# Attention and quantized feed-forward on one core: Newton steps of a layer norm on GpSimd, splits spread over the steps, a pool moved by 128 bytes

## The chip, the cores and the metric

The kernel runs on one core of a Trainium2 chip. The metric is the device time of one execution in microseconds, and a kernel is given by the median of its runs. In the text PE is TensorE (PEld its weight load), DVE is VectorE, ACT is ScalarE, POOL is GpSimd, SP is SyncE, which only issues DMAs here. L150 means line 150 of the kernel before.

## The reference

One transformer block on x [8, 128, 512] in float32: cross attention to a context of the same shape, then a gated feed-forward of 1376 hidden columns whose three weights are quantized to NF4 (4 bits, blocks of 64, scaled by the largest magnitude) and turned back first.

```python
x = x + xattn(layernorm(x), ctx, ctx, mask, Wq, Wk, Wv, Wo)   # 32 query heads, 8 key heads, 128 each,
                                                              # rope, 30 * tanh(logits / 30), softmax
n = layernorm(x)                                              # (x - mean) / sqrt(var + 1e-5), over 512
dq1, dq2, dq3 = (nf4_quant_dequant(w) for w in (w1, w2, w3))
h = silu(n @ dq1.T) * (n @ dq2.T)
out = x + h @ dq3.T
```

## The kernel before

The order of the instructions is written out by hand: each engine carries out its own in the order of the program text, and waits at semaphores for the others.

Every large product takes its float32 operands as two parts, `hi` and `lo`. `split` (L133) makes them: ACT casts `hi`, and DVE or POOL subtracts for `lo`. `product` (L144) then issues three matmuls for each pair, at L148, L149 and L150: hi by lo, hi by hi, lo by hi. The first operand of each is the stationary one.

The program has four stages. First come the keys and values of the context. Then the attention runs in 64 steps `i`, each for one batch and half of a key head's group. Step `i` projects step i-3 (`po`, added by DVE into `acc[b]` at L654; the PSUM buffer `wo` of `po` exists once), transposes and splits the result of step i-2 (`aT`), multiplies weights and values of step i-1 (`pv`, then DVE's reciprocal and `ad` at L642 and L643), and makes the scores of step i (`pl`, tanh and exp on ACT, mask product on POOL at L633).

The second layer norm lies among the last steps. `sums` gives mean and variance of a batch, `finish` the reciprocal root for a pair of batches, `rows` the normalized rows, `turned` transposes them into `xT2`. In `rsqrt` a first guess comes from a shift and a subtraction of the bits, and three Newton steps of three operations each, all on DVE (L100 to L105), on tiles of 128x2. For batches 0 and 1 `finish` and `rows` come at the end of step 60, for 2 and 3 at the end of step 62; batches 4 to 7 follow after the loop.

The feed-forward takes 22 tiles of 24 matmuls (`gate_up`): gate `pg` and up `pu`, for the two halves of the batches and 11 blocks of hidden columns. The first two are issued among the last of the attention; the others are the 20 steps `n` of a loop. Evacuating one means `sg` on ACT (Silu, L700) and `hT` on DVE (L701), one step later. Its weights come by DMAs that POOL's queue issues (`load_w12`, L677) into six buffers with the tag `wq`. The down product `pd` follows: for each batch, `hT` is split by `split_h` into tiles `hs` (also in the six `wq` buffers), four blocks of hidden columns at a time, and multiplied with `w3t`. The 24 splits are in the list `to_split`: three after the last `gate_up`, then one ahead of each of the following entries of `down`.

Beside all this runs a stream of small steps that quantizes the three weights (`quantize`): a POOL normalization (L184), 15 bounds (ACT L174, DVE L180), a last product on DVE (L215 or L257) and the split of the outcome (`store`). `pump(n)` issues as much of it as `n` DVE operations. From step 60 of the attention to the second step of the feed-forward loop none is issued. The tiles of `w3` are the last of the stream; `w3t_0` to `w3t_7` lie in the pool `f1` with `hT` and the output tiles `o`; `w3t_8` and `w3t_9` lie in `nf`, `w3t_10` in `xp`. `f1` is the last pool, and lies where the attention's own pool was.

```python
        if n == last:
            for _ in range(3):
                split_h(*to_split.pop(0))
```

Of the kernel before, what the change touches and what calls it, by code (L numbers as in the profile page):

```python
# [45 lines left out]
def tables():  # L46
    e = np.arange(0, HD, 2, dtype=np.float32)
    inv = (np.float32(1.0) / np.float32(10000.0) ** (e / np.float32(HD))).astype(np.float32)
    phase = np.arange(T, dtype=np.float32)[:, None] * inv[None, :]
    phase = np.tile(phase, (1, 2)).T  # L50
    cos, sin = np.cos(phase).astype(np.float32), np.sin(phase).astype(np.float32)
    sgn = sin.copy()
    sgn[:HD // 2] *= -1
    # A value is above a bound when their difference is above 0, and at most a bound when it is below
    # the next float. The factor makes each such difference larger than any step of the code.
    bias = np.array([np.nextafter(BOUNDS[i], np.float32(np.inf)) if i in NEG else -BOUNDS[i]
                     for i in range(15)] + [0], dtype=np.float32) * np.float32(BIG)
    return (np.ascontiguousarray(np.stack([cos, sgn])),
            np.ascontiguousarray(np.broadcast_to(bias, (P, 16))))
# [3 lines left out]
def block_kernel(ctx: ExitStack, tc: tile.TileContext, x, ctxt, mask, wq, wk, wv, wo, w1, w2, w3, w12t, w3_t,  # L63
# [23 lines left out]
    make_identity(nc, ident)  # L87
    # These bring TensorE to its full clock before the first loads are in.
    warm = bank("pv", "warm")
# [5 lines left out]

# [1 line left out]
    def rsqrt(v, y, n, name):  # L97
        i = tp.tile([P, n], I32, tag="rs_i", name=f"i_{name}")
        t = tp.tile([P, n], F32, tag="rs_t", name=f"t_{name}")
        V.tensor_single_scalar(i, v.bitcast(I32), 1, op=ALU.logical_shift_right)  # L100
        V.tensor_scalar(y.bitcast(I32), i, -1.0, float(0x5F3759DF), ALU.mult, ALU.add)
        for _ in range(3):
            V.tensor_tensor(t, y, y, ALU.mult)
            V.scalar_tensor_tensor(t, t, -0.5, v, ALU.mult, ALU.mult)
            V.scalar_tensor_tensor(y, t, 1.5, y, ALU.add, ALU.mult)  # L105

    class LayerNorm:
        """Of acc[b] for each b of bs: the sums of every b, then finish, then rows of every b."""

# [8 lines left out]

        def finish(self):
            n = len(self.bs)  # L120
            self.y = tp.tile([P, n], F32, tag="ln_y", name=f"y_{self.name}")
            v = tp.tile([P, n], F32, tag="ln_v", name=f"v_{self.name}")
            V.tensor_single_scalar(v, self.mv[:, :, 1], EPS, op=ALU.add)
            rsqrt(v, self.y, n, self.name)

# [5 lines left out]

# [1 line left out]
    def split(hi, lo, src, engine):  # L133
# [3 lines left out]
    def transposed(hi, lo, src, name, tag):  # L137
        """hi + lo = src [T, KT * P] with the columns on the partitions, [P, KT, T]. The split is returned."""
        pt = bank(tag, f"pt_{name}")
        for k in range(KT):  # L140
            E.transpose(pt[:, k * P:(k + 1) * P], src[:, k * P:(k + 1) * P], ident)  # L141
        return lambda: split(hi, lo, pt.rearrange("p (k t) -> p k t", k=KT), V)

    def product(out, pairs, start=True, stop=True):  # L144
        """out = the sum of lhsT.T @ rhs over pairs of (hi, lo), or a part of it."""
        n = len(pairs)
        for i, ((ah, al), (bh, bl)) in enumerate(pairs):
            E.matmul(out, ah, bl, start=start and i == 0, stop=False)  # L148
            E.matmul(out, ah, bh, start=False, stop=False)  # L149
            E.matmul(out, al, bh, start=False, stop=stop and i == n - 1)  # L150

# [1 line left out]
    def scales(a, r, w):  # L153
        """The largest magnitude of each block, and the factor that takes it to 1."""
        V.tensor_reduce(a, blocks(w), AX.X, ALU.max, apply_absolute_value=True)
        V.tensor_single_scalar(r, a, 2.0 ** -126, op=ALU.max)
        V.reciprocal(r, r)
# [4 lines left out]
    class Unit:  # L162
        """Up to 1024 columns of weights, with input channels on the partitions."""
        p = P
# [4 lines left out]
        def bound(self, i):  # L169
            """One more step of the code, from 0 to below, then its sign turned, then from 0 up. The sum is kept  # L170
            in PSUM: an operation of DVE with one operand there leaves GpSimd its port."""
            m = self.tile("nf_m", f"nm_{i}", BF16, 3)
# [16 lines left out]
    class Down(Unit):  # L189
        """Columns h0 to h1 of w3, from its transpose; w3_t has the rows of w3 in the order of (e, p), for 4 * p + e."""  # L190

# [33 lines left out]
    class Up(Unit):  # L225
        """Rows of w1 or w2 or both, from their transposes."""

# [4 lines left out]
        def parts(self, t):  # L232
            """Those of w1 and w2 in t."""
            n = KT * self.r
            return [(j, t[:, i * n:(i + 1) * n].rearrange("p (k h) -> p k h", k=KT)) for i, j in enumerate(self.js)]
# [32 lines left out]
    class Scales:  # L268
        """Those of 128 rows of w1 and of w2, which go to the rows of scale_d."""

# [27 lines left out]
    class Scales3:  # L298
        """Those of w3, of which four rows lie in a partition, a part at a time; and each to the rows of scale3_d
        for its 32 columns: an odd row begins in the middle of a block."""  # L300
        nb = 4 * H // BLK
# [36 lines left out]
    both = [Scales(h) for h in range(NHT)]  # L338
    # What is found in the course of each unit, and when.
    found = {0: [(6, both[2]), (12, both[3])]}  # L340
# [29 lines left out]
    def pump(n):  # L370
        """As much of the stream as n operations of DVE on 1024 columns."""
        credit[0] += n
        while credit[0] > 0:
            credit[0] -= next(stream, n + credit[0])
# [17 lines left out]
    with ExitStack() as c1:  # L392
# [6 lines left out]

# [1 line left out]
        raw_pool = []  # L401
# [12 lines left out]
        def columns(w, h, name):  # L414
            """The columns of one head of w, [P, 2, KT, HD]."""
            raw = stage(w[h], [P, KT, HD], name)
            t = wp.tile([P, 2, KT, HD], F32R, tag="wq", name=name, bufs=6)
            return t, lambda: split(t[:, 0], t[:, 1], raw, V if name == "wk_0" else Q)

        def rope(dst, src, cos, sgn, name, engine=None):  # L420
            """dst = src, in PSUM, turned by its positions; [P, 4, T]. The last step is returned."""
            hd = HD // 2
# [23 lines left out]

# [1 line left out]
        with ExitStack() as c3:  # L448
# [57 lines left out]
            def masks():  # L506
                """1 where a query attends; a query that attends nowhere weighs all keys alike."""
                mf = tp.tile([P, P], F32, tag="xn", name="mf")
# [18 lines left out]

            # The tiles of products, and what else is done in the slot of each.
            tiles = [("k", 0, 0), ("k", 1, 0), ("k", 2, 0), ("k", 0, 1), ("k", 1, 1), ("k", 2, 1),
# [6 lines left out]

            # Weights and context in the order of their use, with the slot that splits them.
            def load_tab(*_):
# [11 lines left out]
            def advance(n):  # L550
                """The splits of slot n, and loads for the next ones as their places come free."""
                while True:
# [47 lines left out]

# [1 line left out]
        at = c1.enter_context(tc.tile_pool(name="at", bufs=2))  # L602
# [67 lines left out]

# [1 line left out]
        w12, hT, ups = {}, {}, []  # L672
# [38 lines left out]
        for i in range(N):  # L711
# [24 lines left out]
            if i == 2:  # L736
                turn(0)
            if 0 <= i - 1:
                values(i - 1)
# [6 lines left out]
            if i in (60, 62):  # L746
                ln.finish()
                xn.update({k: ln.rows(k, ("xn", "t2")[k // 2]) for k in (i - 60, i - 59)})
            for k in due.pop(i, ()):
                todo[k]()  # L750
            if i >= 61:
                load_w12(i - 61)

        project(N - 3)
        turned((2,), "s")
# [20 lines left out]

    f1 = ctx.enter_context(tc.tile_pool(name="f1", bufs=2))
    w3t, hs = {}, {}

# [11 lines left out]
    for n, (half, h) in enumerate(order):  # L791
# [4 lines left out]
        if n in w12_at:  # L796
            load_w12(w12_at[n])
        if n == last:
            for _ in range(3):
                split_h(*to_split.pop(0))  # L800
    evac()
# [61 lines left out]
```

## Time and profile before

| | |
|---|---|
| runs | 811.72, 814.76 and 813.67 us; median 813.67 us |
| profiled execution, span | 813.2 us |
| profiled execution, own time | not listed apart from the span |
| granted TensorE clock, mean | 0.990 |
| busy, PE / DVE / ACT / POOL | 788.0 / 645.0 / 581.1 / 461.7 us |
| attention steps 60 to 63 | about 586 to 610 us |
| last `gate_up` matmul, first `pd` matmul | 740.54 and 743.41 us |

Times in the profile are microseconds from the span's start. A line of the timeline gives start, duration, engine, line, operation, output and inputs, and in brackets the idle time before it with what ended that. Durations of matmuls overlap, so the interval from start to start is the better measure of their pace. In a group's line, after the number of instructions, stand the busy time in all, the mean duration of one in ns, and the idle time before them with its releasers.

### The profile page before, as it was taken

How to read it: one execution, taken by the hardware profiler on the slowest of the kernel's cores; microseconds unless marked ns; L12 is line 12 of the kernel's file. 1: busy time of each engine (PE TensorE's matmuls, PEld its weight loads, DVE VectorE, ACT ScalarE, POOL GpSimd, SP SyncE). 2: the span in 40 equal slices, each digit the busy share in tenths (PEclk: the TensorE clock that was granted, in tenths of full speed). 3: DMA queues.
4: the chain of work that ended last, by engine and by line, in shares of the span. 5: the costliest groups of instructions: out<-in, count | busy, mean ns of one | idle time of the engine just before them, and what ended most of it. 6: DMA issues, size and time to landing. Idle time of an engine off the chain costs nothing.

```text
span 813.2 us, 11144 instructions
## 1 busy us (share of the span) xinstructions
PE 788.0 (97%) x3737; PEld 632.0 (78%) x3737; DVE 645.0 (79%) x876; ACT 581.1 (71%) x820; POOL 461.7 (57%) x370
## 2 busy tenths in 40 slices
PE   8997999999999999999999999999989999998998
PEld 6786877778777787787787887877768888886877
DVE  6748859988888888897888888879877788779941
ACT  6346758779787878888796978898732678669720
POOL 3466636577877777687787787887640223222100
PEclk9998999999999999999999999999999999999999
DMA  6966534736136444616326415331231344341011
GB/s 223 289 170 181 165 95 157 207 106 189 46 110 190 125 135 131 168 54 203 110 99 193 141 39 164 114 111 56 100 108 53 86 147 129 130 160 51 1 65 40
DMA packets 72167, 102.44 MB, mean 126 GB/s; under 512 B 6542, under 2 KB 41678, under 8 KB 72110
## 3 DMA queue, kind: packets, MB, share of 16 engines
q1 hardware_dynamic: 68942, 90.19, 36.3%
q0 software_dynamic: 3168, 11.54, 4.5%
q8 instruction: 30, 0.49, 0.3%
q14 instruction: 27, 0.22, 0.1%
HBM read 79.32 MB, written 22.38 MB: 125 GB/s over the span
## 4 chain that ended last, share of the span: by engine, by line
PE 74%; DVE 7%; DMA 6%; ACT 5%; issue 5%; POOL 2%; SPq 1%; DVEq 0%; POOLq 0%; ACTq 0%
PE po L150 7%; PE po L148 7%; PE po L149 7%; PE pq L148 7%; PE pq L150 7%; PE pq L149 7%; PE pv L640 6%; PE pl L627 6%; DMA s_w<-scale_d 4%; PE pt_a L141 3%; PE pd L150 3%; PE pd L148 3%; PE pd L149 3%; ACT nm_w L174 2%; PE pk L148 1%
## 5 line engine op out<-in xcount | busy, mean ns | idle before, releaser
L180 DVE SCALAR_TENSOR_TENSOR nc_w<-nm_w,nc_w 128x1024 f32<-128x1024 bf16 (+1 forms) x238 | 284.2, 1194 | 65.1 <-ACT nm_w L174 53.8
L174 ACT ACTIVATE nm_w<-w_w,bias 128x1024 bf16<-128x1024 f32 (+1 forms) x255 | 275.6, 1115 | 24.6 <-POOL w_w L184 20.1
L148 PE MATMUL po<-wo,aT 128*128 128x512 f32 x256 | 124.4, 486 | 3.2 <-DVE acc L654 2.4
L430 POOL TENSOR_TENSOR rs_q<-rs_q,sgnq 128x512 f32<-128x512 f32 x64 | 84.0, 1313 | 72.6 <-ACT rs_q L428 71.1
L633 POOL TENSOR_TENSOR th<-th,mt 128x512 f32<-128x512 f32 x64 | 83.7, 1307 | 41.4 <-ACT th L631 27.4
L148 PE MATMUL pq<-xT,wq 128*128 128x512 f32 x256 | 106.0, 414 | 0.3 <-DVE rc_q L429 0.3
L150 PE MATMUL po<-wo,aT 128*128 128x512 f32 x256 | 101.0, 395 | 2.5 <-DVE aT L135 2.5
L150 PE MATMUL pq<-xT,wq 128*128 128x512 f32 x256 | 100.2, 391 | 0.0
L149 PE MATMUL po<-wo,aT 128*128 128x512 f32 x256 | 99.9, 390 | 0.0
L149 PE MATMUL pq<-xT,wq 128*128 128x512 f32 x256 | 99.8, 390 | 0.0
L431 POOL TENSOR_TENSOR qr<-rc_q,rs_q 128x512 f32<-128x512 f32 x56 | 72.6, 1296 | 0.4 <-DVE rs L642 0.4
L640 PEld LDWEIGHTS pv<-vt,th 128*128 128x128 f32 x512 | 66.4, 191 | 4.9 <-POOL th L633 0.6
L148 PEld LDWEIGHTS po<-wo,aT 128*128 128x128 f32 x256 | 48.2, 188 | 27.3 <-issue 12.7
L640 PE MATMUL pv<-vt,th 128*128 128x129 f32 x512 | 67.6, 275 | 0.2 <-POOL th L633 0.2
L627 PE MATMUL pl<-qr,krt 128*128 128x512 f32 x128 | 65.6, 594 | 0.0
L149 PEld LDWEIGHTS po<-wo,aT 128*128 128x128 f32 x256 | 48.2, 188 | 22.0 <-issue 13.8
L427 ACT COPY rs_q<-pq 64x512 f32<-64x512 f32 x64 | 37.3, 582 | 39.2 <-PE pq L150 34.2
L184 POOL TENSOR_TENSOR w_w<-w_w,s_w 128x1024 f32<-128x1024 f32 (+1 forms) x17 | 39.8, 2343 | 44.7 <-DMA s_w<-scale_d 42.9
L630 ACT ACTIVATE th<-pl 128x512 f32<-128x512 f32 x64 | 38.4, 600 | 33.7 <-PE pl L627 33.3
L150 PEld LDWEIGHTS po<-wo,aT 128*128 128x128 f32 x256 | 48.0, 188 | 14.9 <-DVE aT L135 3.8
L150 PEld LDWEIGHTS pq<-xT,wq 128*128 128x128 f32 x256 | 48.0, 188 | 10.8
L148 PEld LDWEIGHTS pq<-xT,wq 128*128 128x128 f32 x256 | 48.2, 188 | 9.8 <-DVE rc_q L429 1.4
(140 smaller groups left out, 1723.6 us busy)
## 6 DMA issues: line engine op xcount, KB each, us to landing
s_w<-scale_d SPq DMA_DIRECT2D x60, 256.0 KB
w12t_d<-dqt SPq DMA_DIRECT2D x22, 512.0 KB
w<-w12t_d POOLq DMA_DIRECT2D x22, 512.0 KB, 4.6
raw_wq<-in_L_xattn_Wq SPq DMA_DIRECT2D x32, 256.0 KB
raw_wo<-in_L_xattn_Wo SPq DMA_DIRECT2D x32, 256.0 KB
ws<-in_L_ffn_w SPq DMA_DIRECT2D x20, 256.0 KB
w_w<-in_w12t SPq DMA_DIRECT2D x10, 512.0 KB
kr_d<-kr SPq DMA_DIRECT2D x16, 256.0 KB
```

The source lines that it names most:

```text
L148: E.matmul(out, ah, bl, start=start and i == 0, stop=False)
L149: E.matmul(out, ah, bh, start=False, stop=False)
L150: E.matmul(out, al, bh, start=False, stop=stop and i == n - 1)
L174: S.activation(m, self.w, AF.Relu, bias=bias[:self.p, i:i + 1], scale=BIG if up else -BIG)
L180: V.scalar_tensor_tensor(self.c, m, step, self.c, ALU.min, ALU.subtract if i == POS[0] else ALU.add)
L184: Q.tensor_tensor(self.w, self.w, self.s, ALU.mult)
L430: Q.tensor_tensor(s, s, every(sgn), ALU.mult)
L431: return lambda: (engine or Q).tensor_tensor(dst, c, s, ALU.add)
L627: E.matmul(pl, krt[kv, u % 2][:, bb * T:(bb + 1) * T], qr[u][:, bb].rearrange("p g t -> p (g t)"), start=True, stop=True)
L630: S.activation(th, pl, AF.Tanh, scale=ATTN_MULT / CAP)
L633: Q.tensor_tensor(em[i], em[i], mt.unsqueeze(1).to_broadcast([P, G, T]), ALU.mult)
L640: E.matmul(pv[:, g, :HD + 1], em[i][:, g], vt[kv][:, b], start=True, stop=True)
```

## The change

- `rsqrt` takes an engine. The shift and the subtraction stay on DVE; where the engine is POOL, each Newton step is four operations (square, times v, times -0.5 plus 1.5, times y), as against three on DVE.
- `finish` of batches 0 and 1 (step 60) and of 2 and 3 (step 62) runs its Newton steps on POOL. The rows of 0 and 1 move from the end of step 60 to step 61, ahead of `values(60)`; those of 2 and 3 from the end of step 62 to the place behind the loop, ahead of `project(61)`. Batches 4 to 7 stay as they were.
- In the feed-forward loop one `split_h` is issued at the end of each of the last four steps, in place of three at the end of the last.
- A tile of 128 bytes a partition, which nothing uses, is taken first from `f1`, so what else lies there moves by 128 bytes.
- Comments are left out.

```diff
-    def rsqrt(v, y, n, name):
+    def rsqrt(v, y, n, name, E=V):
...
         for _ in range(3):
-            V.tensor_tensor(t, y, y, ALU.mult)
-            V.scalar_tensor_tensor(t, t, -0.5, v, ALU.mult, ALU.mult)
-            V.scalar_tensor_tensor(y, t, 1.5, y, ALU.add, ALU.mult)
+            E.tensor_tensor(t, y, y, ALU.mult)
+            if E is V:
+                E.scalar_tensor_tensor(t, t, -0.5, v, ALU.mult, ALU.mult)
+                E.scalar_tensor_tensor(y, t, 1.5, y, ALU.add, ALU.mult)
+            else:
+                E.tensor_tensor(t, t, v, ALU.mult)
+                E.tensor_scalar(t, t, -0.5, 1.5, ALU.mult, ALU.add)
+                E.tensor_tensor(y, y, t, ALU.mult)
...
-        def finish(self):
+        def finish(self, engine=V):
...
-            rsqrt(v, self.y, n, self.name)
+            rsqrt(v, self.y, n, self.name, engine)
...
+            if i == 61:
+                xn.update({k: pair.rows(k, "xn") for k in (0, 1)})
             if 0 <= i - 1:
                 values(i - 1)
...
             if i in (60, 62):
-                ln.finish()
-                xn.update({k: ln.rows(k, ("xn", "t2")[k // 2]) for k in (i - 60, i - 59)})
+                ln.finish(Q)
+                pair = ln
...
+        xn.update({k: pair.rows(k, "t2") for k in (2, 3)})
         project(N - 3)
         turned((2,), "s")
...
     f1 = ctx.enter_context(tc.tile_pool(name="f1", bufs=2))
+
+    f1.tile([P, 32], F32, name="apart_2", bufs=1)
...
-        if n == last:
-            for _ in range(3):
-                split_h(*to_split.pop(0))
+        if n >= last - 3:
+            split_h(*to_split.pop(0))
```

## The prediction

> **What bounds the kernel now.** I read the page's busy shares first, then the stretches of ten microseconds, then each engine in order of time around both places that the change touches.
>
> ```profile
> PE 788.0 (97%) x3737; PEld 632.0 (78%) x3737; DVE 645.0 (79%) x876; ACT 581.1 (71%) x820; POOL 461.7 (57%) x370
> ```
>
> TensorE sets the time; only its idle places and its matmul interval can give time back. Its largest idle place among the stretches:
>
> ```profile
> 740.00:750.00 10.00, 6.33 (x20) 4.44 (x19) 9.69 (x12) 10.00 (x14) 2.20 (x2) 0.83 0.14 44
> ```
>
> Columns: length, then busy time and instructions of PE, PEld, DVE, ACT and POOL, the granted clock, DMA. PE is 3.7 us idle at clock 0.83 while ACT is full; from 720 to 730 ACT was busy for 2.04 us only. PE there, in order of time:
>
> ```profile
> 740.54 0.39 PE L150 MATMUL pu<-xT,w 128*128 128x512 f32 x1
> 743.41 0.47 PE L148 MATMUL pd<-w3t,hs 128*128 128x512 f32 x1 [2.48 <-issue]
> ...
> 745.31 0.76 PE L150 MATMUL pd<-w3t,hs 128*128 128x512 f32 x1 [1.20 <-DVE hs L135]
> ...
> 748.84 0.40 PE L149 MATMUL pd<-w3t,hs 128*128 128x512 f32 x1
> ```
>
> The down product (pd) starts late because the first `hs` casts come at the end of ACT's queue (742.70, below), and its third matmul waits for DVE's half. After that pause the matmuls from 745.87 to 748.43 start 0.43 us apart, at half the granted clock, where 0.23 is usual. The second idle place is the layer norm:
>
> ```profile
> 592.31 1.02 PE L627 MATMUL pl<-qr,krt 128*128 128x512 f32 x2
> 594.22 0.47 PE L148 MATMUL po<-wo,aT 128*128 128x512 f32 x1 [0.89 <-DVE acc L654]
> ...
> 595.65 0.50 PE L150 MATMUL po<-wo,aT 128*128 128x512 f32 x1 [0.73 <-DVE aT L135]
> ```
>
> ```profile
> 589.83 1.24 DVE L104 SCALAR_TENSOR_TENSOR t_y<-t_y,v_y 128x2 f32<-128x2 f32 x1
> ...
> 592.48 1.00 DVE L129 TENSOR_SCALAR xn_y<-acc,mv_y,y_y 128x512 f32<-128x512 f32 x2
> 593.40 0.68 DVE L654 TENSOR_TENSOR acc<-acc,po 128x512 f32<-128x512 f32 x1
> ```
>
> PE's projection waits for DVE's addition into `acc`, which stood behind the Newton steps (589.64 to 592.44) and two rows (1.0 us). The same comes again at 605.20 to 608.29.
>
> **Layer norm on GpSimd.** Off DVE go 9 instructions per finish at an interval of 0.195 us, one of which took 1.24 (it overlapped POOL's mask product, 589.77 to 591.06). The rows move behind the next step's `acc` addition and `aT` split. What is lost now: from pl to the third po takes 1.44 us in the undisturbed step 61 (587.26 to 588.70); here 3.34 (592.31 to 595.65) and 3.09 (605.20 to 608.29): 1.90 + 1.65 = 3.55 us.
>
> POOL gets 12 dependent operations of 128x2 per finish, which the trace lacks. Nearest rows:
>
> ```profile
> L633 POOL TENSOR_TENSOR th<-th,mt 128x512 f32<-128x512 f32 x64 | 83.7, 1307 | 41.4 <-ACT th L631 27.4 <-issue 12.7 <-DVE ad L643 1.0
> ...
> L184 POOL TENSOR_TENSOR w_w<-w_w,s_w 128x1024 f32<-128x1024 f32 x16 | 38.6, 2410 | 39.3 <-DMA s_w<-scale_d 37.5 <-DMA krt<-kr_d 1.8
> ...
> L618 POOL MEMSET vt<- 128x8 f32 x8 | 0.8, 114 | 8.3 <-PE pv L640 8.3
> ```
>
> A line through the first two leaves 0.20 us at no columns; one dependent pair at the start (memset to select, `ident`) shows 0.08 between. I take 0.26, so 3.1 us per finish. The ends are 0.11 (the memset: 1.4 us) and 1.24 (each blocked like that DVE operation: 14.9 us).
>
> First finish: POOL is free when mask product 60 ends, 591.06, and done at 594.2; by then DVE has done `acc` and `aT` and waits; rows 594.25 to 595.25, reciprocal and `ad` of step 60 (0.2 + 0.7) at 596.15. PE's next block, which ended at 598.06, ends at 596.04 without its stall and then wants that `ad`: 0.15 lost. Should POOL's next mask product (1.3 us) read first and block the rows, as a product blocked DVE at 589.83, about 1.1 us more is lost; I don't count it. Queued behind the rows on DVE are that `ad` and the next `acc`; behind the Newton steps on POOL the mask product of step 61, ready at 594.7 anyway, then the two w12 loads (1.25 us), needed only at 616. Second finish, in times 1.9 us earlier: DVE's three operations of it end at 602.3, POOL works to 605.4, the loads to 606.5, mask product 63 to 607.8; PE wants that at 607.7 (611.54 less 1.9 and 1.65, less the wait before it), so 0.2 lost with the wake-up. Gain 3.55 - 0.35 = 3.2 us; both finishes being last, it shrinks by 0.24 us for each 0.01 us more, to nothing at 0.26 + 3.2/24 = 0.39 us.
>
> GPSIMD Engine Reference, section "Engine selection", of the Trainium skill speaks against this: elementwise work with two inputs is about twice as slow there as on VectorE. An estimate by that page, twice DVE's 0.195, makes a finish 4.7 us and this part worth about 0.1 us, the total 3.1 us longer; no trace here shows these shapes on GpSimd.
>
> **One split per step.** ACT, in order of time:
>
> ```profile
> 734.53 0.63 ACT L700 ACTIVATE sg<-pg 128x512 f32<-128x512 f32 x1
> ...
> 742.70 1.65 ACT L134 CAST hs<-hT 128x512 fp32r<-128x512 f32 x3
> ```
>
> The loss now: without it the matmul at 748.84, eleventh of pd, would start at 740.54 + 0.23 + 10 x 0.232 = 743.09, so 5.75 us. Four splits (ACT 0.55 and DVE 0.6 each) go to steps 16 to 19; three stood after step 19. Neither they nor the rows issue a DMA. The first falls into ACT's 0.91 us gap before the sg at 721.81 and DVE's 4.67 us gap before 730.64, both of them waits of the NF4 stream and PE: nothing; without that gap it costs 0.55. The second lands before the sg at 734.53, which PE's last tile (first matmul 735.21) awaits: 0.55 lost. The third and fourth are needed 5.6 and 8.3 us after pd begins; DVE's queue, with one split ahead of each evacuation (735.78 + 0.6 + 0.6 + 3.8 + 0.6; then 0.6 + 3.8 + 0.6), ends them near 741.4 and 746.4. So pd starts at 741.3, with no clock loss: 5.75 - 0.55 = 5.2 us. Next late is `w3t_10`: its POOL half ends at 775.53, on a DVE queue whose work up to there is unchanged; pd needs it 150 matmuls in, at 776.2. Cover of 0.6 us, and it caps any faster pd.
>
> **The 128 bytes.** `apart_2` moves `w3t`, `hT`, `o`. In the program's placement `f1` begins at byte 155392 of a partition, the `wq` buffers with the stationary operand at 112768: 128 apart modulo 256, in pd as in the key product (`cT` also at 155392). The moving operand of gate and up (80000) is level with `wq` modulo 256. Intervals of starts in order of time: 0.232 in pd (749.08 to 764.88 holds 68), 0.231 in the key product, 0.227 in gate and up; `w3t_8` and `w3t_9`, in another pool (48512) and level, run at 0.227 within pd. That is a coincidence of four cases, no mechanism. After the move `w3t` is level too. Gain: 0.0055 x 150 = 0.8, capped at 0.65, and about 0.25 on the last two batches: 0.9 us. Its ends are 0 and 1.2; below zero only if level were worse, which gate and up exclude.
>
> SBUF — State Buffer, section "Who interferes with whom", of the Trainium skill says that PE never waits on anyone for SBUF. By that the move is worth 0 and the sum 0.9 us less.
>
> Comments removed: no instruction.
>
> **Sum.** 3.2 + 5.2 + 0.9 = 9.3. The profile gives no time of its own execution but the span, 813.2, which lies 0.5 under the median of the runs, 813.67 (811.72 to 814.76). Span 803.9; as a median 804.4.
>
> **Rivals.**
> - *GpSimd eats its gain* (0.39 us an operation or more, LN part near 0): 813.67 - 6.1 = 807.6. For it: unmeasured shape. Against: the 0.11 and 0.20 rows. 0.15.
> - *The NF4 stream does not come forward with PE.* The chain of waits runs in the feed-forward through scale DMAs (10.1 us), POOL's normalizing and ACT; if it kept its time, what the layer norm saves is lost at `w3t_10`: 807.6. Against: at 642.67 that chain stems from a PE matmul. 0.10.
> - *The splits do not come early*, as their `wq` buffers free late; with POOL at 0.39 us, no change: 812.7. Against: these held w12_8 and w12_9, last read at 718.9 and 729.8. 0.08.
> - *Slower:* DVE stands behind the rows for POOL and with it `ad`, `acc` and PE, twice. Each 0.1 us of operation above 0.39 costs 2.4 us, so it cancels the other 6.1 near 0.64 and is slower by 0.5% above 0.81; at 1.24 it loses 20 - 6 = 14 us: 828. For it: the 1.24 us collision. 0.05.
>
> **Numbers.** The forecast has 0.62. Half a percent, about what a measurement of this kernel tells from no change, is 4.1 us. Faster 0.62 + 0.15 + 0.10 = 0.87, same 0.08, slower 0.05. Range: best ends 3.55 + 5.75 + 1.2 = 10.5, so 803.2 less the runs' 1.2; up to the two 807.6 rivals plus 0.9: 802.0 to 808.5.
>
> **What would show it.** Right: POOL rows L103 and on at 128x2 near 0.2 us; no idle over 0.3 us before po after 592; pd's first matmul within 1 us of pu's last; clock 1.00 there; pd interval 0.227. Wrong: PE waiting for `ad` or `th` near 596 and 608 (GpSimd), for `w3t` before pd's 151st matmul (stream), or the time leaving faster than 809.6.

## The result, and the profile after

The changed kernel takes 805.01 us (median of 4 runs, 802.15 to 807.59) against 814.07 us (4 runs, 811.72 to 814.76) for the kernel before: ratio 0.9889, 95% interval 0.9868 to 0.9911, or 7.2 to 10.7 us. The four runs of the changed kernel lie in two pairs, 802.15 and 802.80 us and 807.22 and 807.59 us, and the slower pair has the lower granted clock (0.996 and 0.994 against 1.000 and 0.998). The profiled execution of the changed kernel took 807.22 us, with a span of 805.5 us. Its lines are numbered otherwise than those of the kernel before: `product` stands at L153 to L155, `split` at L139 and L140, the normalized rows at L134, the addition into `acc` at L659, `sg` at L705. The page gives the busy shares again:

```profile
PE 784.0 (97%) x3737; PEld 629.8 (78%) x3737; DVE 645.9 (80%) x858; ACT 580.7 (72%) x820; POOL 465.8 (58%) x394
```

The instruction counts are the change: 18 fewer on DVE, 24 more on POOL, none on PE. In the stretch that had held the largest idle place, PE is now full and its clock is whole (columns: length, then busy time and instructions of PE, PEld, DVE, ACT and POOL, clock, DMA):

```profile
730.00:740.00 10.00, 9.30 (x41) 7.39 (x40) 9.58 (x10) 10.00 (x13) 3.12 (x2) 1.00 0.11 42
740.00:750.00 10.00, 10.00 (x45) 8.27 (x45) 9.69 (x11) 9.31 (x13) 1.30 (x1) 1.00 0.17 55
```

PE in order of time, at the start of the down product, the changed kernel:

```profile
732.24 0.39 PE L155 MATMUL pu<-xT,w 128*128 128x512 f32 x1
733.32 0.50 PE L153 MATMUL pg<-xT,w 128*128 128x512 f32 x1 [0.70 <-ACT sg L705]
...
738.68 0.39 PE L155 MATMUL pu<-xT,w 128*128 128x512 f32 x1
738.91 0.39 PE L153 MATMUL pd<-w3t,hs 128*128 128x512 f32 x1
...
741.18 0.39 PE L154 MATMUL pd<-w3t,hs 128*128 128x512 f32 x1
...
772.68 0.39 PE L155 MATMUL pd<-w3t,hs 128*128 128x512 f32 x1
773.67 0.50 PE L153 MATMUL pd<-w3t,hs 96*128 96x512 f32 x1 [0.60 <-POOL w3t L140]
```

Between the last pu and the first pd there is no pause any more, and the eleventh pd (741.18) starts 2.50 us after the last pu, where it was 8.30 before. Two new waits stand in the same list: one for ACT's `sg` before the last gate-and-up tile (1.08 us from start to start where 0.23 is usual) and one for `w3t_10` (0.99). ACT in the same place shows why the first is there, a cast of `hs` between the last NF4 cast and `sg`:

```profile
731.27 1.09 ACT L139 CAST w3t<-w_w 128x512 fp32r<-128x512 f32 x1
732.17 0.62 ACT L139 CAST hs<-hT 128x512 fp32r<-128x512 f32 x1
732.69 0.58 ACT L705 ACTIVATE sg<-pg 128x512 f32<-128x512 f32 x1
```

In the layer norm the Newton steps are on POOL, 12 operations of 0.19 to 0.20 us, each starting 0.277 us after the one before. POOL in order of time, then DVE, then PE:

```profile
590.22 0.20 POOL L103 TENSOR_TENSOR t_y<-y_y 128x2 f32<-128x2 f32 x1
590.50 0.20 POOL L108 TENSOR_TENSOR t_y<-t_y,v_y 128x2 f32<-128x2 f32 x1
...
593.27 0.20 POOL L110 TENSOR_TENSOR y_y<-y_y,t_y 128x2 f32<-128x2 f32 x1
594.00 1.28 POOL L638 TENSOR_TENSOR th<-th,mt 128x512 f32<-128x512 f32 x1 [0.53 <-ACT th L636]
...
607.08 1.30 POOL L638 TENSOR_TENSOR th<-th,mt 128x512 f32<-128x512 f32 x1
```

```profile
590.40 0.69 DVE L659 TENSOR_TENSOR acc<-acc,po 128x512 f32<-128x512 f32 x1 [1.58 <-PE po L155]
...
593.51 2.06 DVE L134 TENSOR_SCALAR xn_y<-acc,mv_y,y_y 128x512 f32<-128x512 f32 x2 [0.89 <-POOL y_y L110]
595.49 0.17 DVE L647 RECIPROCAL rs<-pv 128x4 f32<-128x4 f32 x1
595.70 0.69 DVE L648 TENSOR_TENSOR ad<-pv,rs 128x512 f32<-128x512 f32 x1
...
605.86 2.81 DVE L134 TENSOR_SCALAR xn_y<-acc,mv_y,y_y 128x512 f32<-128x512 f32 x2 [0.77 <-POOL y_y L110]
```

```profile
591.53 1.02 PE L632 MATMUL pl<-qr,krt 128*128 128x512 f32 x2
591.99 0.80 PE L153 MATMUL po<-wo,aT 128*128 128x512 f32 x1
...
596.44 0.65 PE L146 MATMUL pt_a<-ident,ad 128*128 128x128 f32 x4 [1.11 <-DVE ad L648]
```

DVE's addition into `acc` no longer stands behind the Newton steps, and po runs on directly from pl: the old wait is gone. But the two rows take 2.06 us where they took 1.00. The second of them overlaps POOL's mask product (594.00 to 595.28), and PE waits 1.11 us for the `ad` behind them. The rows of batches 2 and 3 take even 2.81 us: the second of them overlaps the two w12 loads that POOL issues (605.76 to 607.06) and the mask product behind these (607.08 to 608.38).

**A ledger.** The time of TensorE's work is compared from the pl of step 60 on (it starts at 587.26 us before and 586.48 after): start of a matmul less the start of that pl, less the same in the profile of before. Earlier differences are left out because the granted clock drops to a half for stretches of 3.4 or 6.8 us near 8, 70 and 105 us, and how many there are differs between two executions of the same kernel: ahead of step 60 they sum to 13.7 us in the profile of before, and to 6.8 and 3.4 us in two profiles of the changed kernel. Whether the change has a part in that, no run shows. Minus is a gain, in us; "LN" is the first pt_y of batch 3 (612.67 us before), behind both finishes, "tile" the last pu matmul.

| kernel | LN | tile | 11th pd | 150th pd | 151st pd | end |
|---|---|---|---|---|---|---|
| changed | -1.96 | -1.07 | -6.87 | -7.67 | -6.91 | -6.93 |
| changed, a second profile | -1.97 | -1.65 | -7.45 | -8.25 | -8.12 | -8.01 |
| layer norm alone | -2.01 | -1.90 | -1.88 | -0.81 | -0.80 | -0.88 |
| splits alone | -0.01 | +0.69 | -5.05 | -4.93 | -4.71 | -4.70 |
| 128 bytes alone | 0.00 | +0.47 | +0.30 | -0.49 | -0.49 | -0.57 |
| changed, no bytes | -2.00 | -1.42 | -7.16 | -7.05 | -6.72 | -6.71 |
| 64 bytes | -1.98 | -1.59 | -7.33 | -7.20 | -7.20 | -7.43 |
| Newton on DVE | -1.78 | -1.03 | -6.83 | -7.62 | -6.81 | -6.75 |
| rows behind `ad` | -3.32 | -3.21 | -9.01 | -9.80 | -8.74 | -8.71 |
| rows behind `ad`, POOL halves | -3.33 | -2.89 | -8.69 | -9.49 | -9.49 | -9.59 |
| rows behind `ad`, splits ahead | -3.29 | -3.01 | -8.81 | -9.61 | -9.61 | -9.67 |
| all three | -3.30 | -2.65 | -8.45 | -9.25 | -9.25 | -9.31 |

Two profiles of one kernel agree to 0.01 us in the layer norm and differ by 0.6 us at the last tile and 1.1 us at the end. So the first column is good to hundredths, the last to about a microsecond. For the changed kernel it says 6.9 and 8.0 us; the medians say 9.1, with an interval that reaches down to 7.2.

### The profile page after: what moved, and what is told of

Its sections match the earlier page's. It is cut to its first block, busy times and chain, and to the rows that moved or that the text cites. A ratio compares the mean times of both kernels' runs of the same rounds, so it can differ in the third digit from the quotient of the medians.

```text
span 805.5 us, 11147 instructions
## 1 busy us (share of the span) xinstructions
PE 784.0 (97%) x3737; PEld 629.8 (78%) x3737; DVE 645.9 (80%) x858; ACT 580.7 (72%) x820; POOL 465.8 (58%) x394
## 4 chain that ended last, share of the span: by engine, by line
PE 70%; DVE 7%; issue 7%; DMA 6%; ACT 5%; POOL 3%; SPq 1%; POOLq 0%; DVEq 0%; ACTq 0%
PE po L155 7%; PE po L153 7%; PE po L154 7%; PE pq L153 7%; PE pq L155 7%; PE pq L154 7%; PE pv L645 7%; PE pl L632 6%; DMA s_w<-scale_d 4%; PE pt_a L146 3%; ACT nm_w L179 2%; POOL w3t L140 1%; DVE nc_w L185 1%; PE pd L153 1%; PE pk L153 1%
## 5 line engine op out<-in xcount | busy, mean ns | idle before, releaser
L153 PE MATMUL po<-wo,aT 128*128 128x512 f32 x256 | 125.1, 489 | 0.7 <-ACT th L635 0.7
L153 PE MATMUL pq<-xT,wq 128*128 128x512 f32 x256 | 106.0, 414 | 0.3 <-DVE rc_q L434 0.3
L155 PE MATMUL po<-wo,aT 128*128 128x512 f32 x256 | 100.8, 394 | 1.7 <-DVE aT L140 1.7
L155 PE MATMUL pq<-xT,wq 128*128 128x512 f32 x256 | 100.2, 391 | 0.0
L153 PEld LDWEIGHTS po<-wo,aT 128*128 128x128 f32 x256 | 48.2, 188 | 23.8 <-issue 12.9
L155 PEld LDWEIGHTS po<-wo,aT 128*128 128x128 f32 x256 | 48.0, 188 | 13.7 <-DVE aT L140 2.4
L155 PEld LDWEIGHTS pq<-xT,wq 128*128 128x128 f32 x256 | 48.1, 188 | 10.8
L153 PEld LDWEIGHTS pq<-xT,wq 128*128 128x128 f32 x256 | 48.2, 188 | 9.8 <-DVE rc_q L434 1.4
```

## The experiments

**The three parts, each alone.** The edit of each kernel is one part of the change put into the kernel before:

```
splits alone:      -        if n == last:              128 bytes alone:  +    f1.tile([P, 32], F32, name="apart_2", bufs=1)
                   -            for _ in range(3):
                   -                split_h(...)        layer norm alone: the changed kernel
                   +        if n >= last - 3:                             with the other two undone
                   +            split_h(...)
```

> The kernel before with the four splits alone. Theory: the late splits cost 5.75 us and the Silu that now queues behind one cast costs PE about 0.5 us, so -5.2 us (ratio 0.994); pd follows pu without a gap at full clock; w3t_10 is in time, since pd keeps its 0.232 us interval. Rival (the pause only moves: PE waits for hs or w3t instead): less than 2 us gained, with PE waiting inside the first 24 pd matmuls.

> The kernel before with the 128 bytes in f1 alone. Theory: pd's interval on w3t_0 to w3t_7 falls from 0.232 to 0.227 us and all else stays; 190 matmuls by 0.0047 give -0.9 us (ratio 0.999), and w3t_10 isn't waited for, as pd still begins at 743. Rival (PE never waits for SBUF): interval 0.232 and 0 us.

> The kernel before with the layer norm's edit alone. Theory: 3.55 us of PE's stalls go, 1.3 us come back at the transposition of step 60 because the two rows run into POOL's mask product, 0.3 us at step 63: about -1.9 us (ratio 0.9977), and the hs casts that hold pd come forward by 1.6 to 1.9 us with it. Rival (the NF4 stream keeps its time): PE is 1.9 us early at 616 and not at 743, 0 us in all.

Measured against the kernel before: splits alone 806.87 us, ratio 0.9914 (0.9881 to 0.9947); 128 bytes alone 812.27, 0.9977 (0.9958 to 0.9996); layer norm alone 810.94, 0.9975 (0.9950 to 1.0000); before 813.44. The splits are most of the gain. The single small parts are at the edge of what the times resolve, so their sizes are read from the ledger: 2.0 us for the layer norm and 0.6 for the bytes. With the splits alone pd follows pu without a pause, as expected, but `w3t_10`, which was expected in time, is waited for by 0.22 us: its POOL half starts 1.08 us later than before, counted from the pl of step 60.

With the layer norm alone the 2 us stand until pd begins and are then halved: PE still pauses there, and in this execution its clock stayed at a half for 6.8 us after the pause instead of 3.4. That pause belongs to what the splits take away, so the loss says nothing of the layer norm.

**The change without the 128 bytes.**

```
-    f1.tile([P, 32], F32, name="apart_2", bufs=1)
```

> The changed kernel without the 128 bytes. Theory: pd's interval is 0.232 again, but the wait for w3t_10 (0.75 us in the changed kernel) is gone, so only about 0.2 us is lost against the changed kernel: -6.9 us against before (ratio 0.9915). Rival (the bytes are worth their full 0.9 us in the changed kernel too): 0.9 us lost and a wait for w3t_10 that stays.

Measured: 806.18 us, ratio 0.9901 (0.9868 to 0.9935). From the eleventh to the 150th pd this kernel loses 0.11 us and the changed one gains 0.80: the bytes do quicken pd. At the end the two kernels differ by 0.2 us in the first profile of the changed kernel and 1.3 in the second. Two things decide that besides the bytes: the last tile, which came 0.35 us later in the first and 0.23 earlier in the second than here, and the wait at `w3t_10`, which took 0.76 and 0.13 us. It was expected to be gone without the bytes; 0.33 us of it are left.

**64 bytes instead of 128, and the other operand moved.** The first gives `apart_2` half its size; the second leaves `f1` as before and moves the `wq` buffers, the stationary operand, by 128 bytes.

```
-    f1.tile([P, 32], F32, name="apart_2", bufs=1)       second, in the kernel before:
+    f1.tile([P, 16], F32, name="apart_2", bufs=1)       +    wp.tile([P, 32], F32, name="apart_w", bufs=1)
```

> The changed kernel with 64 instead of 128 bytes: w3t lies 192 bytes from the wq buffers modulo 256, neither level nor 128 apart. Theory (level is needed): pd's interval near 0.232. Rival (128 apart is the one bad place): 0.227. The time itself moves by less than 0.5 us either way.

> The kernel before with 128 unused bytes in front of the wq buffers, so that w3t moves by 128 bytes as in the change but wq moves with it. Theory (what counts is how the moving operand lies to the stationary one, modulo 256): pd stays at 0.232 us although w3t moved, and gate, up and the query product, whose xT doesn't move, fall from level to 128 apart: 0.232 instead of 0.227, 528 x 0.0055 = 2.9 us and up to 1.8 us more in the query product, 3 to 5 us slower than before (ratio 1.005). Rival (w3t's own place counts): pd at 0.227, gate and up unchanged, 1 us faster.

With 64 bytes the start-to-start interval of pd's 512-column matmuls in its early part is 0.2333 us, the slow one (0.2267 with 128); its single run took 807.90 us. With `wq` moved the time is 817.42 us, ratio 1.0037 (1.0016 to 1.0057), and it is the query, gate and up products that slow down. Groups of instructions by shape, the kernel with `wq` moved (busy time, then mean ns of one):

```profile
L149 PE MATMUL pq<-xT,wq 128*128 128x512 f32 x256 | 101.0, 394 | 0.0
...
L148 PE MATMUL pu<-xT,w 128*128 128x512 f32 x88 | 34.7, 395 | 0.0
L149 PE MATMUL pg<-xT,w 128*128 128x512 f32 x88 | 34.7, 395 | 0.0
```

The same groups of the kernel before had 390, 389 and 389 ns; their starts, 0.227 us apart there, are 0.232 apart here. In that kernel `f1` lies behind `wq` and moves with it, so pd's operands stay 128 apart, and pd stays slow (0.233 at the full clock). So it is not the address of one operand that counts but the distance between the two: level modulo 256 bytes is quick, in pd after the change as in gate and up before; 128 apart is slow, in pd before as in gate and up here; 64 apart (192 the other way) is as slow as 128. What the prediction called a coincidence of four cases is shown for matmuls of 512 columns; the mechanism behind it is not.

**The rows one step later, behind `ad`.**

```
-            if i == 61:
-                xn.update({k: pair.rows(k, "xn") for k in (0, 1)})
             if 0 <= i - 1:
                 values(i - 1)
+            if i == 61:
+                xn.update({k: pair.rows(k, "xn") for k in (0, 1)})
```

> The changed kernel with rows 0 and 1 behind values(60) instead of ahead of it. Theory: in the changed kernel the rows run into POOL's mask product 61 (two rows take 2.06 us for 1.0) and the ad behind them reaches PE 1.26 us late; here ad goes first, that wait is gone and PE is 1.2 us earlier from step 62 to the last gate and up tile. Of this half is lost again at the Silu before the last tile and at w3t_10, since the NF4 stream follows only in part (-1.1 us of 2.0 for the layer norm's own gain): -0.5 to -1.2 us against the changed kernel, ratio to before 0.988. Rival (the rows were late because of POOL's 12 operations, not of the mask product): pt_a waits just the same, 0 us.

DVE in order of time, this kernel:

```profile
593.39 0.69 DVE L648 TENSOR_TENSOR ad<-pv,rs 128x512 f32<-128x512 f32 x1
594.16 2.06 DVE L134 TENSOR_SCALAR xn_y<-acc,mv_y,y_y 128x512 f32<-128x512 f32 x2
```

The rows still take 2.06 us beside a mask product (594.65 to 595.94), but nothing that PE waits for stands behind them. (The rows of batches 2 and 3 still take 2.80 us, and some 0.6 us are lost behind them as in the changed kernel.) PE's wait of 1.11 us is gone and the layer norm part is 3.32 us, against 1.96. At the end it is 1.8 and 0.7 us ahead of the two profiles of the changed kernel, after a wait at `w3t_10` of 1.29 us from start to start. By the clock it is not ahead: 806.06 us, ratio 0.9911 (0.9896 to 0.9925), on another chip than the changed kernel's 805.01. So the 1.36 us are shown where they arise, and not at the end.

**The Newton steps back on DVE, the rows left where the change has them.**

```
-                ln.finish(Q)
+                ln.finish()
```

> The changed kernel with the Newton steps of both finishes back on DVE (nine operations), the rows still moved. Theory: half of the gain comes from moving the rows; with 1.8 us of Newton steps (2.9 with the collision) ahead of acc again, PE waits about 0.9 us in step 61 and 1.2 us in step 63, so the layer norm's part is -1.4 us instead of -2.0: 0.5 us slower than the changed kernel. Rival (GpSimd gives the whole gain): the stalls of before come back, 2 us slower than the changed kernel.

Layer norm part 1.78 us, where 1.4 was expected, against 1.96 with GpSimd; time 806.54, ratio 0.9922 (0.9900 to 0.9944). Moving the rows out of the way of the `acc` addition brings nearly all of that part. DVE, this kernel:

```profile
586.56 1.24 DVE L105 SCALAR_TENSOR_TENSOR t_y<-t_y,v_y 128x2 f32<-128x2 f32 x1
587.83 0.16 DVE L106 SCALAR_TENSOR_TENSOR y_y<-t_y,y_y 128x2 f32<-128x2 f32 x1
...
591.20 1.99 DVE L134 TENSOR_SCALAR xn_y<-acc,mv_y,y_y 128x512 f32<-128x512 f32 x2
```

Here too the rows overlap a mask product (591.48 to 592.90) and take 1.99 us, so the collision comes with the rows' new place and not with GpSimd's Newton steps. What GpSimd adds is 0.2 us as the change stands. Newton steps on DVE together with the rows behind `ad` were not tried, so what GpSimd is worth there stays open.

**A version that keeps what the two waits take.** Four kernels on one chip: the changed kernel again; rows behind `ad`, with the low halves of ten middle `hs` splits on GpSimd ("POOL halves"); rows behind `ad`, with each early split ahead of its step's NF4 work ("splits ahead"); and all three.

```
POOL halves:    -    split(t[:, 0, :n], t[:, 1, :n], hT[...], V)
                +    split(t[:, 0, :n], t[:, 1, :n], hT[...], Q if 4 <= down.index((b, i)) < 14 else V)
splits ahead:   +        if n >= last - 3:
                +            split_h(*to_split.pop(0))
                         pump(3.45 if n > 0 else 0)
                         ...
                -        if n >= last - 3:
                -            split_h(*to_split.pop(0))
```

> The changed kernel once more, so that the other three have it on the same chip. Both theories: its ratio against the kernel before stays within 0.9868 and 0.9911 and its profile shows the same two waits again, about 0.86 us at the sg activation before the last gate-and-up tile and about 0.75 us at w3t_10, before the 151st matmul of pd.

> The changed kernel with the rows behind ad (as in rows_later) and with the low halves of ten of the middle hs splits (fifth to fourteenth) on GpSimd in place of VectorE. Theory (VectorE's queue, 9.69 of 10 us busy from 740 to 750, holds back the NF4 stream and with it w3t_10): the stream's last POOL operation ends at least 2 us earlier against TensorE's work, the wait of 1.06 us at w3t_10 that rows_later shows is gone, and the end lies 9.8 us before that of the kernel before, counted from the pl of step 60 (rows_later: 8.71). Rival (the stream is held by ACT's casts or by its scale DMAs, not by VectorE): the wait at w3t_10 stays between 0.7 and 1.1 us and the end stays at 8.7. Second rival: GpSimd's subtraction (the 96x512 one takes 1.55 us, VectorE's 128x512 one 0.68 to 1.33) ends too late for its own matmuls: pd waits for hs, up to 1 us each.

> The changed kernel with the rows behind ad, and with each of the four early hs splits ahead of the NF4 steps of its gate-and-up step instead of behind them. Theory (a split that stands ahead of the stream's steps meets an idle ACT, and the sg activation before the last tile no longer waits for a cast): no wait over 0.3 us before the last tile, pd starts without a pause; but the wait at w3t_10 takes up what that frees, so the end stays within 0.5 us of rows_later (8.7 us before that of the kernel before). Rival (the casts now hold back the NF4 stream's own ACT work, and w3t_10 comes later still): the wait at w3t_10 grows by the casts' 0.55 us each, up to 2.2, and the end lies 0.5 to 2 us behind rows_later.

> All three: rows behind ad, splits ahead of the NF4 steps, ten low halves on GpSimd. Theory (both waits are made by queues, one of ACT and one of VectorE): no wait over 0.3 us before the last tile nor at w3t_10; the end 9.8 us before that of the kernel before, from the pl of step 60, and 2.5 to 2.9 us ahead of the changed kernel (0.3%). Rival (whatever is freed is taken by the next late transfer or by VectorE's sums at the end): within 0.5 us of rows_pool and of rows_later, and no faster than the changed kernel beyond 1.8 us.

| kernel | median us (runs) | ratio to before, 95% interval |
|---|---|---|
| changed, again | 805.47 (5) | 0.9890 (0.9870 to 0.9911) |
| POOL halves | 803.63 (4) | 0.9870 (0.9845 to 0.9894) |
| splits ahead | 801.43 (4) | 0.9854 (0.9834 to 0.9875) |
| all three | 801.57 (4) | 0.9864 (0.9842 to 0.9887) |

The changed kernel's ratio came out as expected, its two waits did not: 0.33 and 0.13 us above the usual interval, where 0.86 and 0.75 were expected. The NF4 stream runs in steps that wait for a DMA of scales. POOL's normalizing of 1024 columns, in order of time, of the first and then of the second profile:

```profile
668.69 2.39 POOL L189 TENSOR_TENSOR w_w<-w_w,s_w 128x1024 f32<-128x1024 f32 x1 [10.86 <-DMA s_w<-scale_d]
696.06 2.39 POOL L189 TENSOR_TENSOR w_w<-w_w,s_w 128x1024 f32<-128x1024 f32 x1 [10.95 <-DMA s_w<-scale_d]
724.67 2.39 POOL L189 TENSOR_TENSOR w_w<-w_w,s_w 128x1024 f32<-128x1024 f32 x1 [11.14 <-DMA s_w<-scale_d]
```

```profile
665.15 2.40 POOL L189 TENSOR_TENSOR w_w<-w_w,s_w 128x1024 f32<-128x1024 f32 x1 [10.52 <-DMA s_w<-scale_d]
692.77 2.39 POOL L189 TENSOR_TENSOR w_w<-w_w,s_w 128x1024 f32<-128x1024 f32 x1 [10.95 <-DMA s_w<-scale_d]
720.96 2.39 POOL L189 TENSOR_TENSOR w_w<-w_w,s_w 128x1024 f32<-128x1024 f32 x1 [10.74 <-DMA s_w<-scale_d]
```

The three waits sum to 32.95 and 32.21 us; the last of these three stands 0.57 us earlier after the pl of step 60 in the second. That is the size of the difference at the last tile, and the other profiles agree. Take the shift against before, from that pl, of this normalizing and of the last tile. In all eight profiles with early casts behind the stream's work the tile shifts by 0.50 to 0.54 us more to the late side than the normalizing; in the two kernels without early splits (layer norm alone, 128 bytes alone) by 0.02 and 0.03 more; with the splits ahead by 0.24 and 0.31. So the cast costs the last tile half a microsecond, and the rest of the tile's shift is that of the stream, which differs between executions of one kernel. The loss of 0.47 us in the kernel with the 128 bytes alone is of that kind: its normalizing came 0.44 us late.

POOL halves: the last POOL half of `w3t_10` starts 4.3 us earlier after that pl than with rows behind `ad` alone, PE's wait for it is gone, and the end is at -9.59 where -9.8 was expected. The theory that VectorE's queue held `w3t_10` back is borne out. Splits ahead: the interval before the last tile is 0.29 us above the usual, as expected, but the wait at `w3t_10`, which I expected to stay, is gone too; its POOL half starts 1.33 us earlier than with rows behind `ad` alone. PE, and then DVE, in order of time, the kernel with splits ahead:

```profile
769.06 0.39 PE L155 MATMUL pd<-w3t,hs 128*128 128x512 f32 x1
769.29 0.40 PE L153 MATMUL pd<-w3t,hs 96*128 96x512 f32 x1
```

```profile
730.30 0.68 DVE L706 TENSOR_TENSOR hT<-sg,pu 128x512 f32<-128x512 f32 x1
730.90 0.68 DVE L140 TENSOR_TENSOR hs<-hT,hs 128x512 fp32r<-128x512 f32 x1
```

and DVE of the changed kernel:

```profile
733.41 1.11 DVE L140 TENSOR_TENSOR hs<-hT,hs 128x512 fp32r<-128x512 f32 x1
...
745.10 1.33 DVE L140 TENSOR_TENSOR hs<-hT,hs 128x512 fp32r<-128x512 f32 x1
```

The low halves in the changed kernel overlap POOL's products (the first shown a `w3t` product that ends at 733.98, the second a normalizing from 744.58 to 745.88) and take up to 1.33 us; with splits ahead they miss them and take 0.68. Over the first five that is 1.1 us less in the queue that holds the stream than in the changed kernel, and 1.4 less than with rows behind `ad` alone, where two of them take 1.13 and 1.62 us. That is close to the 1.33 by which `w3t_10` comes earlier, but no run moved that collision alone. Between the two profiles of the changed kernel `w3t_10`'s POOL half moves by 1.23 us, and that is the 0.57 of the normalizing and 0.66 of the first five low halves (the fifth took 0.69 in the second profile). All three together bring nothing more (-9.31 against -9.59 and -9.67), as the rival of that run had it, though by medians they lie 3.9 us under the changed kernel, where that rival allowed 1.8; in this profile PE is idle for 0.47 us before the last tile, where at most 0.3 was expected.

The version with splits ahead has the lowest median, though 801.43 is not to be told from the 801.57 of all three: 4.0 us under the changed kernel on the same chip by medians, 3.0 by means (801.40 and 804.35), 2.7 and 1.7 by the ledger. Its interval against before and the changed kernel's overlap slightly (up to 0.9875, and from 0.9870).

## Why the prediction was right, and which terms were off

The time forecast was 804.4 us, and 805.01 came; the sum of 9.3 us compares with 9.1 by the medians and 6.9 or 8.0 by the ledger. The terms, one by one:

- **GpSimd's operation, 0.26 us: 0.277**, so 3.3 us per finish instead of 3.1. The first rival (0.39 and above) is out, and so is the one with GpSimd above 0.64. The Trainium skill's factor of about two for work with two inputs (GPSIMD Engine Reference, section "Engine selection") would have meant 0.39; these 128x2 operations show 0.277 against VectorE's 0.195, a factor of 1.4.
- **The layer norm, 3.2 us: 1.96.** This is the term that failed, and in a place it names: the step "about 1.1 us more is lost; I don't count it", for a mask product that reads first and blocks the rows. It happened: the rows took 2.06 us instead of 1.00, and PE waited 1.11 for `ad` near 596, the sign that I had listed as wrong. Followed along PE, the two stalls of before gave 2.10 + 1.77 = 3.87 us (forecast 3.55), 1.27 was lost at that `ad` (forecast 0.15, from 596.04, which should read 598.06 - 1.90 = 596.16), and 0.64 behind the second finish at `th` and the next pt_y (forecast 0.2), whose rows took 2.81. The rows of the first finish behind `ad` restore 3.32. My own times, the mask product from 594.7 and the rows until 595.25, overlapped; that a VectorE operation beside that product can wait for it was in the trace already, in the 1.24 us operation. The Trainium skill's page SBUF — State Buffer, section "Who interferes with whom", says that a tensor_scalar can take the port pair that GpSimd shares, and that whoever issues second is blocked for the whole instruction. The rows agree in size, 1.06 us lost to a product of 1.28; which issued first the records leave open, since the blocked row starts at 593.97 in them and the product at 594.00.
- **The splits, 5.75 - 0.55 = 5.2: -5.05 alone, and in the changed kernel 5.80 gained from the last pu to the eleventh pd, less 0.89 lost before the last tile (0.32 in the second profile).** The 5.75 was right to 0.05. The loss before the last tile was named, and its 0.55 measures 0.50 to 0.54 once the stream's own shift is taken off; that shift is the rest.
- **Next late: `w3t_10`, cover 0.6 us.** It was next, as named. Its cover did not hold: PE came 7.67 us forward by the 150th pd, and 0.76 of it was given back (0.13 in the second profile). The step that failed is "a DVE queue whose work up to there is unchanged": the low halves of `hs` moved in front of the stream and some of them, beside POOL's products, take up to 1.33 us where 0.6 was counted. The splits alone show it: `w3t_10`'s POOL half, which was to stay where it was, comes 1.08 us later, though the stream's last normalizing of 1024 columns comes only 0.15 later. With ten low halves on GpSimd the wait is gone.
- **The stream comes forward with PE: yes.** Its last normalizing came 1.6 us forward after the pl of step 60, in the second profile 2.2, against 2.0 for PE; the rival in which it kept its time is out. So is the one in which the splits don't come early: the first cast started at 718.20 us in ACT's gap.
- **128 bytes, 0.65 after the cap plus 0.25: 0.80 within pd up to the cap; what is kept of it depends on `w3t_10`, which took back 0.76 in the first profile and 0.13 in the second.** The interval went from 0.232 to 0.227 as said. The 0.25 on the last two batches did not come: from the 151st pd to the end the changed kernel gains 0.02 us. The rule that the prediction set against this term, that PE never waits on anyone for SBUF (same page and section of the Trainium skill), was taken to mean 0; alone the bytes gain 0.79 us from the eleventh to the 150th pd, 0.57 in the ledger to the end and 1.2 by medians, so the measurement decides against that 0. The rule speaks of PE waiting for others; whether the longer interval is a wait at all, no run shows.

The sum came out close because the misses were small beside the one term, the splits, that was right. That the medians agree to 0.6 us is in part luck: 1 to 2 us of the 9.1 lie ahead of step 60 or in the spread between executions and are not explained, and the four runs of the changed kernel spread over 5.4 us.

## What to carry to other kernels

When work is moved from one queue to another, ask what the moved operation will now stand beside, not only what it will stand behind: the rows left the place ahead of the `acc` addition and met GpSimd's mask product, and 1.00 us became 2.06. It matters where in its engine's queue a split stands, and what is then under way beside it: the same four splits, moved across one call, removed the wait at `w3t_10`. A path that is next late and is fed by DMAs has a spread of its own, 0.57 us here between two profiles at the stream's last normalizing, and a cover of 0.6 is no cover against it.

## What the runs showed of the hardware

The start-to-start interval of 128x512 matmuls depends on where the two operands lie: 0.2267 us with moving and stationary operand level modulo 256 bytes, 0.232 to 0.233 with 128 bytes between them, in the query, gate, up and down products, and 0.233 with 64 in the down product. For the 256-column matmuls of the last batch no such rule shows: 0.118 to 0.119 us at 128 bytes, 0.119 to 0.120 level, 0.115 at 64 bytes in its one profile. After PE's pause at the start of pd in the kernel before (2.48 us, and 1.20 us two matmuls later) the clock was granted at a half for 3.4 us, with the layer norm alone (2.46 and 1.19 us) for 6.8, and with `wq` moved already after 1.34 and 1.19 us for 3.4.
